# Edge indices loaded first, constants and the first normalization moved into the third counting pass

## The chip, the core and the metric

The kernel runs on one core of a Trainium2 chip, as one launch. The metric is the device time of that core in microseconds, the median of three runs.

The engines are named as in the profile: PE is TensorE (matmuls), PEld its weight loads, DVE is VectorE, ACT is ScalarE, POOL is GpSimd, SP is SyncE, which here only issues transfers. Each engine works through its own queue of instructions in order; an instruction whose inputs are not there holds everything behind it on that engine.

## What is computed

The reference is a network of four layers over a graph of 512 nodes with 768 features and 8704 edges. Each layer normalizes the nodes, adds a graph part and an attention-like part, and then a feed-forward part with experts:

```python
edge_index = jnp.stack([src, dst])
xn = _layernorm(x, axis=-1)
x = x + _L0_gnn_ref(xn, edge_index, edge_attr_256, ...) + _L0_mix_ref(xn[None], ...)[0]
x = x + _L0_ffn_ref(_layernorm(x, axis=-1)[None], ...)[0]
...
x = x + _L3_gnn_ref(xn, ..., src, dst) + _L3_mix_ref(xn[None], ...)[0]
x = x + _L3_ffn_ref(_layernorm(x, axis=-1)[None], ...)[0]
return x
```

The edges are drawn with replacement, so two nodes can be joined by several edges, of several types. What the graph parts need of the edges is therefore a table of counts: how many edges of each type go from node s to node d. The first stage of the kernel makes these tables, and sums the 256 features of the edges that arrive at each node.

## The kernel before

`Net.__init__` (L166 to L219) issues the load of the nodes x (L179, 1.5 MB) and of a table of small columns (L181) from GpSimd, and makes constants: an identity matrix, three stacked 32 x 32 identities `sel` (L188), the identity in bf16 `identb` (L205), a comparison mask `lower` (L214), node numbers `number` (L217, L219), matrices of ones, small columns. GpSimd fills some of them, VectorE casts or compares the others. The stages that read `sel`, `identb`, `lower` and `number` come after the counting.

`counts` (L363) makes the tables. Four loads bring the edges' sources, destinations and two types to the tile `raw` (named `so` in the profile, since it shares that buffer; L383). L384 casts all four to f32 as `ind`; L391 to L393 make from the types three weights per edge, `worth`, in which two counts share one f32 number (one of them times 4608). Edges lie 128 to a step, 68 steps in all. For each step j, VectorE compares a row of numbers 0 to 511 with the destination, which gives a one-hot tile `ohd` (L457, made once, kept for all passes), and with the source, times each of the three weights, which gives `so` (L460, three instructions, three buffers). TensorE multiplies the two and sums over the steps.

There are four counting passes: for each half of the sources (h = 0, 1), for each half of the steps (g = 0, 1). A pass has 34 steps with six matmuls each (L463, 204 matmuls) into six PSUM banks, which are first preset by a small matmul (L454). After each pass the six sums are copied out (L234 on VectorE, L236 on ScalarE, in turn), split into high and low parts (L470, L476, L477), and `features` (L402) follows for eight or nine groups: SP loads edge features (L406), ScalarE and VectorE split them into three bf16 parts (L408 to L411, two buffers each for `ea` and `part`), and TensorE multiplies them with `ohd` (L416). After the second and the fourth pass `finish` (L421) adds the halves and sends the tables to memory.

After `counts`, `tile_net` calls `net.norm(net.x, xn)` (L1817), the first normalization: for each quarter of the nodes two statistics instructions (L351), an aggregation (L352), a square root on ScalarE (L353), a reciprocal (L354), and the scaled copy (L355). L355 writes a tile that lies where the counting's tiles lie, so it can run only after them; the other instructions have no such bound. A scheduler orders each engine's queue by what is ready and by priority; so before, the statistics and the constants stood at the front of VectorE's queue, ahead of L384.

In the last stage, `ffn3` (L1570), scores go through a sigmoid on ScalarE (L1605) and are then ranked on VectorE (L1617 to L1622). A dummy sigmoid on one column (L1585) is there to have the sigmoid's table loaded ahead; as it depends only on a small constant, the scheduler had put it at the start of the program.

ScalarE also issues transfers there: the normalized rows of x go to memory as `f_there` (L1461), and three of the six transposed tiles `xnT` are copied out by it (L236).

Of the kernel before, what the change touches and what calls it, by code (L numbers as in the profile page):

```python
# [10 lines left out]
F32 = mybir.dt.float32  # L11
BF16 = mybir.dt.bfloat16
I16 = mybir.dt.int16
# [7 lines left out]
P = 128  # L21
N = 512
# [142 lines left out]
class Net:  # L165
    def __init__(self, ctx, tc, dram, at, out):  # L166
        self.tc, self.nc, self.d, self.at, self.out = tc, tc.nc, dram, at, out
        nc = self.nc
        self.cw = ExitStack()
        self.wp = self.cw.enter_context(tc.tile_pool(name="wp", bufs=6, side="right"))  # L170
        self.keep = ctx.enter_context(tc.tile_pool(name="keep", bufs=1))
        self.small = ctx.enter_context(tc.tile_pool(name="small", bufs=4))
        self.rowp = self.cw.enter_context(tc.tile_pool(name="rowp", bufs=2, side="right"))
        self.pp = ctx.enter_context(tc.tile_pool(name="pp", bufs=8, space=PSUM))
        self.dp = ctx.enter_context(tc.tile_pool(name="dp", bufs=1, space=DRAM))
        self.turn = 0
        keep = self.keep
        self.x = keep.tile([P, NT, D], F32, name="x")
        nc.gpsimd.dma_start(self.x, dram["x"].rearrange("(t p) d -> p t d", p=P))  # L179
        self.cols = keep.tile([P, dram["cols"].shape[1]], F32, name="cols")  # L180
        nc.gpsimd.dma_start(self.cols, dram["cols"])  # L181
        self.ident = keep.tile([P, P], F32, name="ident")
        make_identity(nc, self.ident)


        self.sel = keep.tile([96, 32], BF16, name="sel")
        for i in range(3):
            nc.vector.tensor_copy(self.sel[32 * i : 32 * i + 32, :], self.ident[:32, :32])  # L188
# [16 lines left out]
        nc.vector.tensor_copy(self.identb, self.ident)  # L205
        self.big0 = keep.tile([P, 1], F32, name="big0")
        nc.gpsimd.memset(self.big0, -BIG)
        self.onesb = keep.tile([P, P], BF16, name="onesb")
        nc.gpsimd.memset(self.onesb, 1.0)
        self.lower = keep.tile([P, P], BF16, name="lower")  # L210
        with tc.tile_pool(name="init", bufs=1) as ip:
            io = ip.tile([P, P], F32, name="io")
            nc.gpsimd.iota(io, pattern=[[1, P]], base=0, channel_multiplier=0, allow_small_or_imprecise_dtypes=True)
            nc.vector.tensor_scalar(self.lower, io, self.me, None, OP.is_gt)  # L214

        self.number = keep.tile([P, NT, 2], BF16, name="number")
        nc.vector.tensor_copy(self.number[:, :, 0], self.me.to_broadcast([P, NT]))  # L217
        for t in range(NT):
            nc.gpsimd.memset(self.number[:, t, 1:2], float(t * P))  # L219


    def ps(self):
# [121 lines left out]
    def norm1(self, x, out, t):  # L344

        nc = self.nc
        st = self.small.tile([P, 2, 6], F32, name="st")
        mv = self.small.tile([P, 2], F32, name="mv")
        r = self.small.tile([P, 1], F32, name="rs")
        for h in range(2):  # L350
            nc.vector.bn_stats(st[:, h, :], x[:, t, h * HW : (h + 1) * HW])  # L351
        nc.vector.bn_aggr(mv, st)  # L352
        nc.scalar.activation(r, mv[:, 1:2], AF.Sqrt, bias=self.eps)  # L353
        nc.vector.reciprocal(r, r)  # L354
        nc.vector.tensor_scalar(out[:, t, :], x[:, t, :], mv[:, 0:1], r, OP.subtract, OP.mult)  # L355

# [6 lines left out]
    def counts(self, c0, g0):  # L363
# [10 lines left out]
        with ExitStack() as c:  # L374
# [5 lines left out]
            ind = one.tile([P, 4, EJ], F32, name="ind")  # L380
            raw = sp.tile([P, 4, EJ], I32, name="so")
            for n, a in enumerate(("src", "dst", "edge_type_3", "edge_type_4")):
                nc.gpsimd.dma_start(raw[:, n, :], d[a].rearrange("(p j) -> p j", p=P))  # L383
            nc.vector.tensor_copy(ind, raw)  # L384


# [3 lines left out]
            for n, ((e, u), (f, v)) in enumerate((((3, 0), (3, 1)), ((3, 2), (3, 3)), ((2, 0), (2, 1)))):  # L390
                nc.vector.tensor_scalar(worth[:, n, :], ind[:, f, :], float(v), BASE, OP.is_equal, OP.mult)  # L391
                nc.vector.tensor_scalar(add, ind[:, e, :], float(u), None, OP.is_equal)
                nc.vector.tensor_add(worth[:, n, :], worth[:, n, :], add)  # L393
            io = one.tile([P, N], I16, name="io")
            nc.gpsimd.iota(io, pattern=[[1, N]], base=0, channel_multiplier=0)
            below = self.rowp.tile([1, D], BF16, name="mid", bufs=1)[:, :N]
            nc.vector.memset(below, -START)
            ohd = one.tile([P, EJ, N], BF16, name="ohd")
# [3 lines left out]
            def features(q):  # L402


                ea = ep.tile([P, 2, 256], F32, name="ea")
                nc.sync.dma_start(ea, attr[:, 2 * q : 2 * q + 2, :])  # L406
                part = ep.tile([P, 3, 2, 256], BF16, name="part")
                nc.scalar.copy(part[:, 0], ea)  # L408
                nc.vector.tensor_sub(ea, ea, part[:, 0])
                nc.scalar.copy(part[:, 1], ea)  # L410
                nc.vector.tensor_sub(part[:, 2], ea, part[:, 1])  # L411
                for i in range(2):
                    j = 2 * q + i
                    for n in range(3):
                        for f in range(2):
                            nc.tensor.matmul(eft[f], part[:, n, i, f * P : (f + 1) * P], ohd[:, j, :],  # L416
                                             start=j == 0 and n == 0, stop=j == EJ - 1 and n == 2)
# [31 lines left out]
            for h in range(2):  # L449
                digit = {}  # L450
                for g in range(2):
# [3 lines left out]
                    for j in range(g * HJ, (g + 1) * HJ):  # L455
                        if h == 0:
                            nc.vector.tensor_scalar(ohd[:, j, :], io, ind[:, 1, j : j + 1], None, OP.is_equal)  # L457
                        so = sp.tile([P, 3, 256], BF16, name="so")
                        for n in range(3):
                            nc.vector.tensor_scalar(so[:, n, :], io[:, h * 256 : (h + 1) * 256], ind[:, 0, j : j + 1],  # L460
                                                    worth[:, n, j : j + 1], OP.is_equal, OP.mult)
                        for (t, n), p in acc.items():
                            nc.tensor.matmul(p, so[:, n, t * P : (t + 1) * P], ohd[:, j, :], start=False,  # L463
                                             stop=j == (g + 1) * HJ - 1)
                    for (t, n), p in acc.items():
                        s = dg.tile([P, N], F32, name="s")
                        self.copy(s, p)
                        part = dg.tile([P, N], F32, name="part")

                        nc.scalar.activation(part, s, AF.Identity, scale=1.0 / BASE, bias=self.shift)  # L470
                        lo, hi = s, part
                        if g == 0:
                            hi = dg.tile([P, N], I16, name=f"hi{t}{n}", bufs=1)
                            lo = dg.tile([P, N], I16, name=f"lo{t}{n}", bufs=1)
                            digit[t, n] = lo, hi
                        nc.vector.tensor_scalar(hi, part, MAGIC, -MAGIC, OP.add, OP.add)  # L476
                        nc.vector.scalar_tensor_tensor(lo, hi, -BASE, s, OP.mult, OP.add)  # L477
                        if g == 1:
                            finish(h, t, n, lo, hi, *digit[t, n])

                    for q in range((2 * h + g) * EJ // 8, (2 * h + g + 1) * EJ // 8):
                        features(q)
# [1087 lines left out]
    def ffn3(self, xn, xnT, there):  # L1570
# [5 lines left out]
        with ExitStack() as c:  # L1576
# [5 lines left out]
            self.wp = c.enter_context(tc.tile_pool(name="f3_w", bufs=10, side="right"))  # L1582

            first = self.small.tile([P, 1], F32, name="r3")
            nc.scalar.activation(first, self.eps, AF.Sigmoid)  # L1585
            io = one.tile([P, P], F32, name="io")
            nc.gpsimd.iota(io, pattern=[[1, P]], base=0, channel_multiplier=0, allow_small_or_imprecise_dtypes=True)
            number = one.tile([P, NT, 2], F32, name="number")
# [208 lines left out]
def tile_net(ctx, tc, dram, at, out, only=ALL):  # L1797
# [10 lines left out]
    with ExitStack() as ck, ExitStack() as c0:  # L1808
# [4 lines left out]
        with tc.tile_pool(name="L0", bufs=1) as pool:  # L1813
            xnT = pool.tile([P, KC, N], F32, name="xnT")
            with tc.tile_pool(name="L0n", bufs=1) as p2:
                xn = p2.tile([P, NT, D], F32, name="xn")
                net.norm(net.x, xn)  # L1817
                net.to_fm(xn, xnT)
            if "mix0" in only:
                net.mix0(xnT)  # L1820
# [61 lines left out]
```

## Time and profile before

| what | value |
|---|---|
| median of 3 runs | 4313.59 us (4308.73 to 4316.22) |
| profiled execution, its own time | 4315.56 us |
| its span, first to last instruction | 4313.8 us |
| granted TensorE clock, mean | 0.986 |
| first counting matmul (L463) | 26.3 us |
| first pass ends, last pass ends | 72.6 us, 287.8 us |
| first normalized transposes (L317) | 338.9 us |
| loads of weights of the last stage (Wg, Wu, Wd) | 128 each, 1152 KB each |

In the timeline a line has its start, its busy time, the engine, the program line, the operation, output and input with sizes, and a count; in brackets stands how long the engine had been idle before it and what ended that. A busy TensorE is not one at its peak rate, since matmuls are pipelined.

### The profile page before, as it was taken

How to read it: one execution, taken by the hardware profiler on the slowest of the kernel's cores; microseconds unless marked ns; L12 is line 12 of the kernel's file. 1: busy time of each engine (PE TensorE's matmuls, PEld its weight loads, DVE VectorE, ACT ScalarE, POOL GpSimd, SP SyncE). 2: the span in 40 equal slices, each digit the busy share in tenths (PEclk: the TensorE clock that was granted, in tenths of full speed). 3: DMA queues.
4: the chain of work that ended last, by engine and by line, in shares of the span. 5: the costliest groups of instructions: out<-in, count | busy, mean ns of one | idle time of the engine just before them, and what ended most of it. 6: DMA issues, size and time to landing. Idle time of an engine off the chain costs nothing. (4 is left out here: it accounts for less than half of the span.)

```text
span 4313.8 us, 40131 instructions
## 1 busy us (share of the span) xinstructions
PE 4125.5 (96%) x16376; PEld 2099.9 (49%) x16376; DVE 1305.0 (30%) x3120; ACT 650.1 (15%) x1233; POOL 270.3 (6%) x316
## 2 busy tenths in 40 slices
PE   7989999999988999999999999978989999999998
PEld 3434555554444666755644444444554444444443
DVE  7772111112332125623220101035752122122211
ACT  2121200001211223421200000012610000000000
POOL 1120000001022010000000000021100000000000
PEclk9999999999989999999999999989999999999999
DMA  3111011111047112211211111063069999999998
GB/s 110 52 62 56 22 44 66 66 55 53 20 178 269 44 63 71 99 52 46 105 43 66 44 56 55 0 255 129 12 257 419 419 420 420 420 417 420 419 421 362
DMA packets 98956, 710.30 MB, mean 165 GB/s; under 512 B 12032, under 2 KB 12097, under 8 KB 29393
## 3 DMA queue, kind: packets, MB, share of 16 engines
q1 hardware_dynamic: 77776, 601.13, 35.1%
q0 software_dynamic: 16512, 93.97, 5.8%
q10 hardware_dynamic: 4480, 12.58, 0.8%
q8 instruction: 132, 2.16, 0.2%
q14 instruction: 56, 0.45, 0.0%
HBM read 685.09 MB, written 22.54 MB: 164 GB/s over the span
## 5 line engine op out<-in xcount | busy, mean ns | idle before, releaser
L1724 PE MATMUL ps<-w,xg 128*64 128x384 f32 x3072 | 566.0, 489 | 4.2 <-DMA w<-in_f_Wg_dram 2.1
L1724 PEld LDWEIGHTS ps<-w,xg 128*64 128x64 f32 x3072 | 234.1, 137 | 296.2 <-issue 271.1
L1356 PE MATMUL ps<-aT,w 128*128 128x512 f32 x864 | 372.3, 592 | 0.0
L1740 PE MATMUL ps<-w,hT 128*64 128x384 f32 x1536 | 320.7, 490 | 7.4 <-DMA w<-in_f_Wd_dram 3.1
L312 PE MATMUL ps<-xnT,w 128*128 128x512 f32 (+1 forms) x732 | 322.6, 598 | 0.2 <-ACT xnT L236 0.2
L1356 PEld LDWEIGHTS ps<-aT,w 128*128 128x128 f32 x864 | 164.2, 190 | 203.6 <-issue 202.3
L360 DVE TENSOR_TENSOR x<-x,ps 128x384 f32<-128x384 f32 x240 | 131.6, 552 | 329.6 <-PE ps L312 259.6
L312 PE MATMUL ps<-w,xnT 128*128 128x384 f32 x672 | 221.7, 486 | 0.2 <-DVE xnT L234 0.2
L312 PEld LDWEIGHTS ps<-xnT,w 128*128 128x128 f32 (+1 forms) x732 | 134.5, 185 | 175.9 <-issue 172.4
L1740 PEld LDWEIGHTS ps<-w,hT 128*64 128x64 f32 x1536 | 131.9, 136 | 170.8 <-issue 145.0
L312 PE MATMUL ps<-w,hT 128*128 128x384 f32 x552 | 189.4, 499 | 8.8 <-ACT hT L850 8.8
L312 PE MATMUL ps<-C,parts 128*128 128x512 bf16 x864 | 188.8, 380 | 2.5 <-DVE inv L1378 2.5
L463 PE MATMUL ps<-ohd,so 128*128 128x512 bf16 x816 | 182.1, 383 | 2.8 <-DVE so L460 2.8
L312 PEld LDWEIGHTS ps<-w,xnT 128*128 128x128 f32 x672 | 127.0, 190 | 88.6 <-issue 4.8
L1366 DVE TENSOR_TENSOR aT<-inv,ps 128x512 f32<-128x512 f32 x72 | 49.4, 686 | 365.7 <-PE ps L312 365.7
L1727 ACT ACTIVATE h<-ps 128x384 f32<-128x384 f32 x64 | 31.4, 490 | 794.0 <-PE ps L1724 794.0
L1728 DVE TENSOR_TENSOR h<-h,ps 128x384 f32<-128x384 f32 x64 | 35.4, 553 | 376.5 <-PE ps L1724 369.3
L312 PEld LDWEIGHTS ps<-w,hT 128*128 128x128 f32 x552 | 105.4, 194 | 83.9 <-ACT hT L850 13.7
L312 PE MATMUL ps<-w,aT 128*128 128x384 f32 (+1 forms) x416 | 139.6, 486 | 0.5 <-DVE aT L234 0.4
L312 PEld LDWEIGHTS <-parts 128*128 128x128 bf16 x864 | 84.8, 98 | 108.1 <-issue 8.8
L312 PE MATMUL ps<-xnT,sw 128*128 128x512 f32 x288 | 136.7, 605 | 0.0
L460 DVE TENSOR_SCALAR so<-io,ind,worth 128x256 bf16<-128x256 int16 x408 | 121.7, 356 | 35.6 <-PE ps L463 35.5
(487 smaller groups left out, 4787.7 us busy)
## 6 DMA issues: line engine op xcount, KB each, us to landing
w<-in_f_Wg_dram SPq DMA_DIRECT2D x128, 1152.0 KB, 14.5
w<-in_f_Wu_dram SPq DMA_DIRECT2D x128, 1152.0 KB, 14.4
w<-in_f_Wd_dram SPq DMA_DIRECT2D x128, 1152.0 KB, 15.2
w<-in_g_w_dram SPq DMA_DIRECT2D x54, 1152.0 KB, 5.1
w<-in_m_wqkv_dram SPq DMA_DIRECT2D x24, 1152.0 KB, 6.7
w<-in_g_t_dram SPq DMA_DIRECT2D x12, 1152.0 KB, 5.6
w<-in_m_wp_dram SPq DMA_DIRECT2D x8, 1152.0 KB, 5.3
ea<-in_edge_attr_dram SPq DMA_DIRECT2D x34, 256.0 KB, 2.7
```

What stands on the lines that cost most here:

```text
L312: self.nc.tensor.matmul(out, a, b, start=n == 0, stop=n == len(pairs) - 1)
L360: self.nc.vector.tensor_add(xs, xs, p)
L460: nc.vector.tensor_scalar(so[:, n, :], io[:, h * 256 : (h + 1) * 256], ind[:, 0, j : j + 1], worth[:, n, j : j + 1], OP.is_equal, OP.mult)
L463: nc.tensor.matmul(p, so[:, n, t * P : (t + 1) * P], ohd[:, j, :], start=False, stop=j == (g + 1) * HJ - 1)
L1356: nc.tensor.matmul(outs[nb * 3 + f], w[:, k, f * P : (f + 1) * P], xT[:, k, :], start=first and k == 0, stop=last and k == KC - 1)
L1366: nc.vector.tensor_mul(aT[:, f, :], inv[:, r, :], p)
L1724: nc.tensor.matmul(p[a * 64 : a * 64 + 64, :HW], xg[:, k, a * CAP : (a + 1) * CAP], ws[b][a][:, k, :], start=k == 0, stop=k == KC - 1)
L1727: nc.scalar.activation(h, pg[:, :HW], AF.Silu)
L1728: nc.vector.tensor_mul(h, h, pu[:, :HW])
L1740: nc.tensor.matmul(po[nb][a * 64 : a * 64 + 64, :HW], hT[:, f * P + a * 64 : f * P + a * 64 + 64], wd[a][:, f, nb * HW : (nb + 1) * HW], s ...
```

## The change

Four things are changed.

- The four index loads are issued by SP (src and edge_type_3) and ScalarE (dst and edge_type_4) in place of GpSimd. In both queues they stand first.
- GpSimd makes the matrix of ones `onesb` and the row of numbers `io` before it issues the loads of x and of the columns. `io` is one tile of 512 int16 for all uses; the separate f32 row of 128 for `lower` and the row in `counts` are gone.
- The VectorE instructions that make `sel`, `identb`, `lower` and `number` are in a new function `constants`. It and the first normalization are put behind the last `so` instruction of the third pass (h = 1, g = 0) and the last second-part copy issued until then (`issue_after`). In the queue of VectorE the constants then stand directly behind that `so`, the statistics between the evacuation of the third pass and the features that follow; of ScalarE's four roots and the load of their table likewise. The scaled copies L355 stay where they were.
- The dummy sigmoid is put behind the last root of the last normalization.

On TensorE the order of matmuls changes in two places: two of the first features' matmuls come after the first pass in place of inside it, and after the third pass some presets and the first four matmuls of the fourth pass stand among the features. On the other engines nothing behind the first normalization changes but the place of the dummy sigmoid, with its table load, which replaces the one at L1605.

```diff
         self.x = keep.tile([P, NT, D], F32, name="x")
+        self.cols = keep.tile([P, dram["cols"].shape[1]], F32, name="cols")
+
+        self.onesb = keep.tile([P, P], BF16, name="onesb")
+        nc.gpsimd.memset(self.onesb, 1.0)
+        self.io = keep.tile([P, N], I16, name="io")
+        nc.gpsimd.iota(self.io, pattern=[[1, N]], base=0, channel_multiplier=0)
         nc.gpsimd.dma_start(self.x, dram["x"].rearrange("(t p) d -> p t d", p=P))
-        self.cols = keep.tile([P, dram["cols"].shape[1]], F32, name="cols")
         nc.gpsimd.dma_start(self.cols, dram["cols"])
...
-        for i in range(3):
-            nc.vector.tensor_copy(self.sel[32 * i : 32 * i + 32, :], self.ident[:32, :32])
...
-        nc.vector.tensor_copy(self.identb, self.ident)
...
-        self.onesb = keep.tile([P, P], BF16, name="onesb")
-        nc.gpsimd.memset(self.onesb, 1.0)
...
-            io = ip.tile([P, P], F32, name="io")
-            nc.gpsimd.iota(io, pattern=[[1, P]], base=0, channel_multiplier=0, allow_small_or_imprecise_dtypes=True)
-            nc.vector.tensor_scalar(self.lower, io, self.me, None, OP.is_gt)
...
-        nc.vector.tensor_copy(self.number[:, :, 0], self.me.to_broadcast([P, NT]))
...
+    def constants(self):
+
+        nc = self.nc
+        for i in range(3):
+            nc.vector.tensor_copy(self.sel[32 * i : 32 * i + 32, :], self.ident[:32, :32])
+        nc.vector.tensor_copy(self.identb, self.ident)
+        nc.vector.tensor_scalar(self.lower, self.io[:, :P], self.me, None, OP.is_gt)
+        nc.vector.tensor_copy(self.number[:, :, 0], self.me.to_broadcast([P, NT]))
...
-        nc.scalar.activation(r, mv[:, 1:2], AF.Sqrt, bias=self.eps)
+        self.root = nc.scalar.activation(r, mv[:, 1:2], AF.Sqrt, bias=self.eps).ins
...
-                nc.gpsimd.dma_start(raw[:, n, :], d[a].rearrange("(p j) -> p j", p=P))
+                (nc.sync, nc.scalar)[n % 2].dma_start(raw[:, n, :], d[a].rearrange("(p j) -> p j", p=P))
...
-            io = one.tile([P, N], I16, name="io")
-            nc.gpsimd.iota(io, pattern=[[1, N]], base=0, channel_multiplier=0)
+            io = self.io
...
-                nc.scalar.copy(part[:, 1], ea)
+                made["part"] = nc.scalar.copy(part[:, 1], ea)
...
-                            nc.vector.tensor_scalar(so[:, n, :], io[:, h * 256 : (h + 1) * 256], ind[:, 0, j : j + 1],
+                            made["so"] = nc.vector.tensor_scalar(so[:, n, :], io[:, h * 256 : (h + 1) * 256], ind[:, 0, j : j + 1],
...
+                    if h == 1 and g == 0:
+
+                        self.begun = made["so"].ins, made["part"].ins
...
-            nc.scalar.activation(first, self.eps, AF.Sigmoid)
+            with self.tc.issue_after(self.root):
+                nc.scalar.activation(first, self.eps, AF.Sigmoid)
...
-                net.norm(net.x, xn)
+                with tc.issue_after(net.begun[0]), tc.issue_after(net.begun[1]):
+                    net.constants()
+                    net.norm(net.x, xn)
```

More of the change, by code (lines that the diff above doesn't have):

```diff
@@ L204, in __init__ @@
         self.identb = keep.tile([P, P], BF16, name="identb")
-        nc.vector.tensor_copy(self.identb, self.ident)
         self.big0 = keep.tile([P, 1], F32, name="big0")
         nc.gpsimd.memset(self.big0, -BIG)
-        self.onesb = keep.tile([P, P], BF16, name="onesb")
-        nc.gpsimd.memset(self.onesb, 1.0)
         self.lower = keep.tile([P, P], BF16, name="lower")
-        with tc.tile_pool(name="init", bufs=1) as ip:
-            io = ip.tile([P, P], F32, name="io")
-            nc.gpsimd.iota(io, pattern=[[1, P]], base=0, channel_multiplier=0, allow_small_or_imprecise_dtypes=True)
-            nc.vector.tensor_scalar(self.lower, io, self.me, None, OP.is_gt)
         self.number = keep.tile([P, NT, 2], BF16, name="number")
-        nc.vector.tensor_copy(self.number[:, :, 0], self.me.to_broadcast([P, NT]))
         for t in range(NT):
             nc.gpsimd.memset(self.number[:, t, 1:2], float(t * P))
+    def constants(self):
[5 more added lines that the diff above has]
+        nc.vector.tensor_copy(self.number[:, :, 0], self.me.to_broadcast([P, NT]))
     def ps(self):
```

## The prediction

> **What bounds the kernel now.** I read the table of engines first, then the chain of waits, then a table of stretches over the first 342 us, then the timeline of those stretches.
>
> ```profile
> PE 4125.5 (96%) x16376; PEld 2099.9 (49%) x16376; DVE 1305.0 (30%) x3120; ACT 650.1 (15%) x1233; POOL 270.3 (6%) x316
> ```
>
> TensorE is busy for 96% of the span, so a change pays where TensorE has nothing to do. The stretches show where that is in the part that the change touches (columns: stretch, length, busy time of PE, PEld, DVE, ACT and POOL, granted clock, DMA share, GB/s):
>
> ```profile
> 0.00:25.50 25.50, 2.73 (x6) 0.80 (x7) 12.48 (x36) 7.59 (x12) 13.27 (x32) 1.00 0.93 352
> 25.50:72.60 47.10, 47.09 (x208) 20.09 (x208) 46.11 (x179) 0.59 (x1) 0.00 (x0) 1.00 0.04 16
> 179.00:217.60 38.60, 38.60 (x181) 17.47 (x180) 26.27 (x90) 1.90 (x4) 0.00 (x0) 1.00 0.06 16
> 217.60:249.30 31.70, 29.23 (x129) 11.64 (x127) 24.16 (x42) 14.32 (x24) 7.75 (x8) 1.00 0.23 67
> ```
>
> The first 25.5 us hold six preset matmuls, 2.73 us. From there the counting passes keep TensorE full: the first to 72.6, the third to 217.6. Between the third and the fourth (217.6 to 249.3) it loses 31.70 - 29.23 = 2.5 us, and VectorE is busy for 24.16 of 31.70. The timeline of the start says what TensorE waits for:
>
> ```profile
> 16.09 1.48 DVE L351 BATCH_NORM_STATS2 st<-x 128x6 f32<-128x384 f32 x3 [9.15 <-DMA x<-in_x_dram]
> ...
> 20.24 1.97 DVE L188 CAST sel<-ident 32x32 bf16<-32x32 f32 x3
> ...
> 22.23 1.56 DVE L205 CAST identb<-ident 128x128 bf16<-128x128 f32 x1
> ...
> 24.23 0.28 DVE L384 CAST ind<-so 128x272 f32<-128x272 int32 x1
> ...
> 25.51 1.01 PE L416 MATMUL ps<-ohd,part 128*128 128x512 bf16 x2 [17.17 <-DVE ohd L457]
> ```
>
> VectorE stands 9.15 us on the 1.5 MB of x, then does the nodes' statistics and the constants, and only then the indices (24.23), their one-hot rows (L457, 25.11), and the first counting matmul. Nothing before L384 is needed by the counting. One other place is touched, at the start of the last stage:
>
> ```profile
> 3179.18 1.28 ACT L1605 ACT_TABLE_LOAD   x1 [5.72 <-issue]
> 3180.47 0.22 ACT L1605 ACTIVATE sc<-ps 128x64 f32<-128x64 f32 x1
> ...
> 3180.75 1.09 PE L317 MATMUL ps<-ident,sc 128*128 128x128 f32 x8 [1.64 <-ACT sc L1605]
> ```
>
> ScalarE loads the sigmoid's table when the scores are already there, and the ranking waits for it. The dummy sigmoid of L1585, meant for this, ran at 20.67 us.
>
> **The Trainium skill.** "ScalarE: Activation LUTs", What ACT_TABLE_LOAD costs, gives about 1283 ns for a load of any set; the trace has 1283 ns, ten times for L353 alone. "DMA: Bandwidth & Descriptors", Issuing engine by pattern, calls the sync and scalar queues generally faster than GpSimd's; here a 256 KB load from SP took 2.7 us in the median, the four 34 KB index loads from GpSimd 10.9 to 11.6 us, but these stood behind x. Its Specifications ask for 512 B per descriptor for full rate; an index row has 68 x 4 = 272 B, and no row of this trace shows such rows alone on a hardware queue. "GPSIMD Engine Reference", 1. Specifications, says that GpSimd's memory interfaces are shared with VectorE; the trace agrees: 18 instructions of L460 beside GpSimd's bias work took 8.02 us at 244.56, 0.446 each, and 0.86 for three, 0.287, elsewhere.
>
> **Part 1, the indices first.** SP and ScalarE each issue two of the four index loads before everything else. An SP issue takes 0.42 (0.85 for two), so src and edge_type_3 leave at 0.73 and 1.15, dst and edge_type_4 at about 0.72 and 1.1. At the 2.7 us of the first edge features they land by 3.8; this is an estimate from that row, with 1.7 (the 3 KB rows' median) and 12.0 us (the slowest features load, behind weights) as its ends. Behind them on SP the features move by 2 x 0.42 and land at 3.46 + 0.84 = 4.3; g_we and the weights move likewise, needed first at 328. ScalarE's table load moves by about 0.8, to end near 2.9, before 4.3. On GpSimd the ones and the 512-wide iota (0.20 and 0.59) go ahead of x and cols, needed first at 215 and 331 now.
>
> The order of VectorE's queue is: L384, nine instructions of worth (24.54 to 26.63 less the L457 and L460 between them, 1.05 us), L409 twice, L411 twice, then the first L457. L384 has a new wait on two queues, and everything named stands behind it. So 3.8 + 0.3 + 1.05 = 5.1; the features' pair, there at 4.3 plus 0.65 for L408, ends 2.82 us after it begins (4.11 to 6.93 before): 7.9. First one-hot at 7.9 where it was 25.1: 17.2 us earlier. TensorE's half-speed start costs the same as before (matmuls 0.43 apart from 25.5 to 29.2, 0.217 after). The loop orders two matmuls of L416 after the pass which stood in it. I take -17.0, with -18.5 (indices and features sooner) and -13.0 (indices at 8).
>
> GpSimd's bias work (L269, L270, 18.69 to 23.7) stays, but now falls into the first pass: 5 us at 0.287/0.446 costs VectorE 1.8 us. Three tiles of so, 3 x 1.30 us of matmuls, cover it: nothing, 1.8 if VectorE has no lead.
>
> **Part 2, constants and normalization after the last so of the third pass.** That so is done at 214.77 of the old clock. Behind it now: sel, identb, lower, number, which took 3.74 us (20.24 to 23.98), with GpSimd working beside them to 23.7. In the third pass GpSimd does nothing (its L271 waits until 241), so I price them at the 0.20 between L214 and L217: six, 1.2 us. The statistics run from 16.09 to 20.24, 4.15, plus 0.25 for reciprocals: 4.4. Together 5.6 us, at most 8.1. ScalarE gets one table load and four roots: 1.28 + 4 x 0.29 = 2.4; a root waits for its statistics, and behind it stand L470 and L408.
>
> VectorE's idle time from 214.77 to 249.30 is 2 x 0.44 + 31.70 - 24.16 = 8.4 us, enough in sum but mostly after 229. Before that, constants and first statistics (1.2 + 1.0) less 0.88 idle push the evacuation of the six sums by 1.3; the further statistics among L409 and L411 add 0.7, 0.6 and 1.2: the third later features group is some 3.8 us late. Features go through two buffers (L408 at 230.17, 235.73, 241.17: 5.5 us for two groups, where TensorE needs 24 x 0.217 = 5.2), so a delay is handed on; one later idle of 0.68 between L409 and L411 takes part of it. The 2.05 us that TensorE lost after 245.4 come back only in part, since GpSimd's L271 to L273 now run beside the features. I take +3.0; the ends are 0 (all in idle time) and +8.0 (all on the path). The statistics leave no gap where they were: nothing else stood before L384.
>
> **Part 3, the sigmoid's table.** The dummy now follows the last root (3170.45). 1.28 go from the path at 3179. The dummy's 1.28 + 0.20 stand ahead of the last f_there issue (3171.39) and three copies of xnT (3171.89): those move by about 0.5, and the gate's six-step sums by up to 0.4. SP's next loads wait 6.3 us for f_there, but are covered by queued weights (DMA share 1.01 from 3175 to 3200). The next weights wait for TensorE's first experts (DMA 0.11 in 3200 to 3205), so time gained here reaches the end: -0.9, ends -1.3 and 0.
>
> **Sum.** -17.0 + 3.0 - 0.9 = -14.9. The profiled execution took 4315.56, its span 4313.8 (1.8 around it): 4300.7 for it. It is 2.0 above the median 4313.59, so the median goes to 4298.7; I say 4299. Beyond 342 us only the sigmoid's place differs in the five engines' orders, so an earlier start carries through.
>
> **Rivals.** *The features ring takes it all*: VectorE has no useful idle time before 229; against it, most of the added work falls later. -17.0 + 8.0 - 0.9 = -9.9: 4303.7.
>
> *Late indices*: the short rows land after 12 us. Then L384 at 13.1, worth to 14.4, the features' pair 2.8: 17.2, a gain of 7.9, net -5.8: 4307.8. For it: 272 B rows, four queues' worth of traffic at 352 GB/s. Against: they are first on idle engines.
>
> *Slower, the ring at half speed*: if each L409 and L411 had to wait for a root or a statistic, and each statistic for ScalarE, the two-group period would go from 5.5 to 11 us; four periods cost 22: -17.0 + 22.0 - 0.9 = +4.1, 4317.7. It decides from a period of 10.0, where 4 x 4.5 eats the 17.9 gained. Against it: only a few of the later features instructions have one in front.
>
> *The move doesn't happen*: a scheduler could have placed the constants early again; the queue's order shows them after the so's, so I give that nothing.
>
> **Numbers.** Forecast 0.75, ring takes all 0.13, late indices 0.08, ring at half speed 0.04. About 0.2%, 8.6 us, can be told from no change: faster below 4305. Faster: 0.75 + two thirds of 0.13 = 0.84; same 0.12; slower 0.04. The range takes the bounds together: -18.5 + 0 - 1.3 = -19.8 and -13.0 + 7.0 - 0 = -6.0: 4293 to 4308, which holds the first two cases and half of the third.
>
> **What would show it.** First L457 at 7 to 9 us and counting matmuls from 8.2 to 55 without a gap; L384 waiting on an index DMA that lands before 5. Casts of sel near 0.2 each, not 0.66, after 195. From the end of the third pass to the fourth pass's steady run, 34 to 36 us where it was 31.7. No table load at L1605. It is wrong if L384 starts after 8, if TensorE's loss in that stretch is above 8 us, or if the shift measured at 342 us is not there at 3160.

## The result, and the profile after

The median is 4300.56 us (4295.38 to 4303.31, 11 runs) where the kernel before took 4312.43 beside it on the same chip (4307.29 to 4316.22, 11 runs): ratio 0.9974, 95% interval 0.9965 to 0.9982. That is 11.9 us less, with 8 to 15 from the interval. A second measurement of the same kernel gave 4301.86 against 4309.53, ratio 0.998 (0.9971 to 0.9988): 7.7 us less, with 5 to 12.5 from its interval. The forecast was 14.9 us less.

The profiled execution of the changed kernel took 4295.38 us, its span is 4293.4, so its profile lies 20.4 us below that of before: 9.7 at the first transposes, 7.3 between these and the last stage, 1.4 from there to the experts, 2.0 after. Only the first and the third are used below; experiment 8 says why the second is not, and the last stays open.

The first line of the page answers to the one shown of before:

```profile
PE 4115.2 (96%) x16376; PEld 2091.7 (49%) x16376; DVE 1304.4 (30%) x3120; ACT 648.2 (15%) x1232; POOL 269.9 (6%) x311
```

Work and shares are as they were. Stretches of the changed kernel that answer to those of before (stretch, length, busy time of PE, PEld, DVE, ACT and POOL, clock, DMA share, GB/s):

```profile
0.00:11.40 11.40, 2.71 (x6) 0.89 (x7) 4.89 (x15) 3.65 (x5) 5.82 (x23) 1.00 0.82 293
11.40:62.90 51.50, 50.18 (x206) 18.43 (x206) 50.24 (x178) 0.79 (x2) 4.96 (x4) 1.00 0.30 124
...
208.10:239.80 31.70, 29.80 (x130) 11.77 (x129) 27.82 (x62) 16.73 (x29) 9.61 (x8) 1.00 0.23 60
```

The empty start is 11.4 us long instead of 25.1. But the first pass, which took 47.5 us from the first one-hot row before, takes 51.5, and has 4.96 us of GpSimd work in it where it had none. The stretch after the third pass, with the constants and statistics now in it, is no worse: TensorE is busy for 29.80 of 31.70 us, before for 29.23, although VectorE's busy time there rose from 24.16 to 27.82.

The timeline of the start (the lines of the changed kernel stand 3 to 7 further down: L388 is L384 of before, L411 to L414 are L408 to L411, L460 is L457, L463 is L460, L466 is L463):

```profile
0.73 0.41 ACTq L387 DMA_DIRECT2D so<-in_dst_dram  x1
0.73 0.38 SPq L387 DMA_DIRECT2D so<-in_src_dram  x1
...
1.49 0.93 POOL L185 DMA_DIRECT2D x<-in_x_dram  x1
1.64 0.90 SPq L409 DMA_DIRECT2D ea<-in_edge_attr_dram  x2
...
4.23 0.43 DVE L388 CAST ind<-so 128x272 f32<-128x272 int32 x1 [2.85 <-DMA so<-in_edge_type_dram]
...
6.25 0.68 DVE L412 TENSOR_TENSOR ea<-ea,part 128x512 f32<-128x512 f32 x1
8.79 0.62 ACT L411 CAST part<-ea 128x512 bf16<-128x512 f32 x1 [3.24 <-DMA ea<-in_edge_attr_dram]
...
9.44 0.69 DVE L412 TENSOR_TENSOR ea<-ea,part 128x512 f32<-128x512 f32 x1 [2.51 <-ACT part L411]
10.05 1.46 DVE L414 TENSOR_TENSOR part<-ea,part 128x512 bf16<-128x512 f32 x2
...
11.43 0.35 DVE L460 TENSOR_SCALAR ohd<-io,ind 128x512 bf16<-128x512 int16 x1
```

The indices are there at 4.2 and the weights `worth` at 6.25, so a one-hot row could begin then. The time of `worth` does not hang on the landing of the indices. In a second profile of the same kernel (experiment 8) they are there 0.7 us earlier:

```profile
3.49 1.16 DVE L388 CAST ind<-so 128x272 f32<-128x272 int32 x1 [2.12 <-DMA so<-in_edge_type_dram]
```

The cast takes 1.16 us in place of 0.43, and ends at 4.66 in both profiles, 0.16 after GpSimd's fill of `bias`, which runs from 3.09 to 4.50 in both; VectorE's next work after `worth` begins at 6.25 and 6.24.

In VectorE's queue the first two features groups stand ahead of it. The second group's load, which landed in time before, can be used only from 8.79; ScalarE splits it, VectorE subtracts, and the first one-hot row comes at 11.43.

Milestones in us (a pass ends with the last matmul of its long row):

| kernel | first one-hot row | first pass ends | third ends | first transposes |
|---|---|---|---|---|
| before | 25.11 | 72.62 | 217.76 | 338.87 |
| changed | 11.43 | 62.91 | 208.29 | 329.19 |

13.7 us are gained at the first one-hot row, 9.7 at the end of the first pass, and 9.7 at the first transposes.

### The profile page after: what moved, and what is told of

Same layout as the page of the kernel before. It is cut to its first block, busy times and chain, and to the rows that moved or that the text cites. A ratio compares the mean times of both kernels' runs of the same rounds, so it can differ in the third digit from the quotient of the medians.

```text
span 4293.4 us, 40119 instructions
## 1 busy us (share of the span) xinstructions
PE 4115.2 (96%) x16376; PEld 2091.7 (49%) x16376; DVE 1304.4 (30%) x3120; ACT 648.2 (15%) x1232; POOL 269.9 (6%) x311
## 5 line engine op out<-in xcount | busy, mean ns | idle before, releaser
L466 PE MATMUL ps<-ohd,so 128*128 128x512 bf16 x816 | 184.3, 383 | 2.6 <-DVE so L463 2.5
L1734 ACT ACTIVATE h<-ps 128x384 f32<-128x384 f32 x64 | 31.4, 491 | 793.7 <-PE ps L1731 793.7
L466 PEld LDWEIGHTS <-so 128*128 128x128 bf16 x816 | 77.8, 98 | 115.0 <-DVE so L463 28.7
```

The lines of the kernel that those rows point to most:

```text
L1734: nc.scalar.activation(h, pg[:, :HW], AF.Silu)
```

## Experiments

Each kernel is the changed one with an edit. Each was timed beside the kernel before on the same chip (4310.65 us for experiments 1 to 4, 4309.94 for 5 to 8, 4309.53 for the last two runs), and is compared through it. Lines of an edited kernel may be shifted by one to eight.

| experiment | first one-hot row | first pass ends | third ends | first transposes | median | ratio to before |
|---|---|---|---|---|---|---|
| 1 bias work later | 12.00 | 59.53 | 205.80 | 326.43 | 4297.69 | 0.997 (0.9959 to 0.9981) |
| 2 one-hot rows spread | 11.46 | 59.52 | 204.90 | 325.72 | 4296.21 | 0.9967 (0.9955 to 0.998) |
| 3 features later | 6.25 | 57.96 | 203.98 | 324.75 | 4293.36 | 0.9961 (0.9947 to 0.9974) |
| 4 all three | 6.25 | 53.41 | 200.69 | 321.51 | 4292.41 | 0.9959 (0.9946 to 0.9973) |
| 5 x issued later | 8.33 | 60.40 | 205.71 | 326.30 | 4298.77 | 0.9974 (0.9964 to 0.9984) |
| 6 indices as before | 19.19 | 70.51 | 215.96 | 336.57 | 4308.14 | 0.9999 (0.999 to 1.0008) |
| 7 constants not held | 11.38 | 64.50 | 211.41 | 332.39 | 4304.44 | 0.9984 (0.9977 to 0.9991) |
| 8 sigmoid as before | 11.34 | 62.90 | 208.25 | 329.96 | 4302.27 | 0.9983 (0.9976 to 0.9989) |

### 1. GpSimd's bias work out of the first pass

Why does the first pass take 4 us longer? The timeline of the changed kernel, VectorE's and GpSimd's lines:

```profile
11.69 0.85 DVE L463 TENSOR_SCALAR so<-io,ind,worth 128x256 bf16<-128x256 int16 x3
...
12.72 1.49 DVE L463 TENSOR_SCALAR so<-io,ind,worth 128x256 bf16<-128x256 int16 x3
13.31 0.81 POOL L273 CAST bias<-row 1x768 bf16<-1x768 f32 x1 [6.92 <-DMA row<-in_m_bv_dram]
14.21 1.75 POOL L274 TENSOR_TENSOR row<-row,bias 1x768 f32<-1x768 f32 x1
...
14.39 4.13 DVE L463 TENSOR_SCALAR so<-io,ind,worth 128x256 bf16<-128x256 int16 x3
15.92 0.81 POOL L273 CAST bias<-row 1x768 bf16<-1x768 f32 x1
16.81 1.63 POOL L274 TENSOR_TENSOR row<-row,bias 1x768 f32<-1x768 f32 x1
```

Three `so` instructions take 0.85 us alone; beside GpSimd's subtractions they take 4.13, and the triple before 1.49. The excess is 3.28 + 0.64 = 3.9 us. The experiment lets GpSimd's arithmetic on the bias rows begin only after a tile of the second pass:

```diff
-        self.parts(out, t[:1, :n], t[:1, :n], mid[:, :n], [self.nc.gpsimd.tensor_copy] * 3, self.nc.gpsimd.tensor_sub)
+        with self.tc.issue_after(self.gate):
+            self.parts(out, t[:1, :n], t[:1, :n], mid[:, :n], [self.nc.gpsimd.tensor_copy] * 3, self.nc.gpsimd.tensor_sub)
...
+                        if h == 0 and j == HJ + 5:
+                            gate = self.small.tile([1, 1], BF16, name="gate")
+                            self.gate = nc.gpsimd.tensor_copy(gate, so[:1, 0, :1]).ins
```

> GpSimd's arithmetic on the two bias rows is held until the second counting pass; all else is as in the changed kernel. GpSimd theory (its bias work at 13.3 to 18.5 us keeps VectorE from the so tiles, and VectorE has no slack in the first pass): the first pass ends near 58.9 us instead of 62.75, the median falls by 3 to 4 us to about 4297. Pace theory (VectorE's own queue, with the one-hot rows of all 68 steps in the first pass, sets the pace, and GpSimd beside it adds little): the pass still ends at 62 or later, median 4300. Traffic theory (the 400 GB/s of x and weights until 25 us slow the engines): no change either, since the transfers stay.

In its timeline the third triple, and with it all others of the pass, is back at 0.85:

```profile
14.32 0.85 DVE L464 TENSOR_SCALAR so<-io,ind,worth 128x256 bf16<-128x256 int16 x3
```

The pass takes 59.53 - 12.00 = 47.5 us, as in the kernel before. So the 4.0 us go with GpSimd's work: the loads beside the pass and the earlier start are still there without it. One more thing differs between the profiles. TensorE's matmuls stand 0.43 us apart at first and 0.22 later, and this slow start lasts 3.7 us before, 5.7 in the changed kernel and 3.9 here. It is not what made the pass longer: in the second profile of the changed kernel it lasts 4.2, and the pass takes 51.4 all the same. Of the 4.0 us, 2.8 are left at the first transposes; 0.6 went into a later first row, and the stretch from the first to the third pass's end is 0.9 longer, where the bias work now lies.

### 2. The same bias work, with room beside it

The program makes the one-hot rows of the second pass ahead, in the first: two or three `ohd` rows between the triples. Here each row waits for the `so` of the step before it, so that a pass makes only its own:

```diff
-                            nc.vector.tensor_scalar(ohd[:, j, :], io, ind[:, 1, j : j + 1], None, OP.is_equal)
+                            with tc.issue_after(made["so"].ins) if j else ExitStack():
+                                nc.vector.tensor_scalar(ohd[:, j, :], io, ind[:, 1, j : j + 1], None, OP.is_equal)
```

> Each one-hot row is queued behind the so of the step before, so that only 34 of 68 are made in the first pass. GpSimd's bias work stays where it is. GpSimd theory and pace theory both: VectorE gets 6 to 9 us of slack in the first pass and makes up for the loss; the pass ends near 58.5 us instead of 62.75, the second pass stays at about 44 us, median near 4297. Traffic theory: the pass still ends at 62.5.

The collision is all there, in the timeline of this kernel:

```profile
15.26 1.75 POOL L274 TENSOR_TENSOR row<-row,bias 1x768 f32<-1x768 f32 x1
...
15.44 4.14 DVE L464 TENSOR_SCALAR so<-io,ind,worth 128x256 bf16<-128x256 int16 x3
```

Yet the pass takes 48.1 us. VectorE's busy time in it is 43.8 us of 48.1, against 50.2 of 51.5 in the changed kernel. So nearly all that the collision costs the pass, it costs because rows that nobody needs yet have taken VectorE's spare time. Here TensorE idles 0.21 us once, at 19.63, and then runs 116 matmuls in 25.64 us, 0.221 each; in the changed kernel it idles 0.57 and 0.27 and then runs 108 in 25.40, 0.235 each, at VectorE's pace.

### 3. The first features behind step 20

```diff
-                nc.vector.tensor_sub(ea, ea, part[:, 0])
-                made["part"] = nc.scalar.copy(part[:, 1], ea)
-                nc.vector.tensor_sub(part[:, 2], ea, part[:, 1])
+                with tc.issue_after(made["early"]) if q < 2 else ExitStack():
+                    nc.vector.tensor_sub(ea, ea, part[:, 0])
+                    made["part"] = nc.scalar.copy(part[:, 1], ea)
+                    nc.vector.tensor_sub(part[:, 2], ea, part[:, 1])
...
+                        if h == 0 and j == 20:
+                            made["early"] = made["so"].ins
```

> VectorE's and ScalarE's splits of the first two features groups are queued behind step 20 of the first pass. Theory that the first one-hot row waits in VectorE's queue behind these four instructions, and they wait for the second features load, landing at 8.8 us: first one-hot row at 6.3 us in place of 11.4. As the pass is bound by VectorE, only the wait of 2.5 us is saved, not the 2.9 us of work: the pass ends near 60.3 us, median about 4298. Rival, that TensorE alone bounds the pass: it ends 5 us sooner, at 57.7, median 4295.5. If the index loads themselves were late, the first one-hot row stays at 11.

The first row comes at 6.25, straight after `worth`, 5.2 us earlier; so those 5.2 us were the features' pair: 2.5 of waiting for the second load, the rest its work. The pass ends at 57.96, near the rival's 57.7, not at my 60.3: I had expected the pair's 2.8 us of VectorE to be paid later in the same pass. VectorE is busy for all 51.7 us from the first row to the pass's end, where in the changed kernel 1.3 of 51.5 are idle. What took up the rest of the 2.8 was not tried.

### 4. All three edits

> The three together. If the three causes are right and TensorE is then the bound of the first pass: first one-hot row at 6.3 us, pass ended at 53 to 54.5 us, 8 to 9.5 us sooner than in the changed kernel, median 4291 to 4293. If something else holds the pass, transfers or TensorE's half-speed start, it ends at 57 or later and the median is 4296 or more.

First row at 6.25, and the pass takes 47.2 us. The transposes come 7.7 us before those of the changed kernel, 17.4 before those of the kernel before. It consists of the three edits above and nothing else. It was run again beside the unaltered changed kernel:

> The version with all three edits (bias arithmetic in the second pass, one-hot rows one step ahead, first features' splits behind step 20), beside the changed kernel in one job. Transposes stand 7.7 us earlier than in the changed kernel (321.5), and nothing later differs in order: the median is 7 to 8 lower than the changed kernel's of this job, 17 to 19 lower than the kernel before. If the gain is lost downstream, less than 4.

Median 4290.61 (4290.23 to 4292.13), ratio to before 0.9957 (0.9943 to 0.997), where the changed kernel has 4301.86 and 0.998 (0.9971 to 0.9988). The two medians are 11.2 apart, more than the 7 to 8 expected, the two profiles' transposes 8.8 (320.34 and 329.12). I take the transposes for the edits' effect, since nothing later differs in order. They have a spread of their own: the two profiles of this version differ by 1.2 us there (321.51 and 320.34). The first row is at 6.25 in both, but TensorE's slow start lasts 4.8 us in one and 2.9 in the other, and at half the pace 1.9 us more cost about 0.95, which is the difference at the end of the first pass (53.41 and 52.47). This version beats both kernels: in this measurement its five runs all lie below every run of the two.

### 5. x issued behind GpSimd's constants

Was it x that held up the second features load? The 1.5 MB are issued at 3.79 here instead of 1.49:

```diff
-        nc.gpsimd.dma_start(self.x, dram["x"].rearrange("(t p) d -> p t d", p=P))
-        nc.gpsimd.dma_start(self.cols, dram["cols"])
...
             nc.gpsimd.memset(self.number[:, t, 1:2], float(t * P))
+        nc.gpsimd.dma_start(self.x, dram["x"].rearrange("(t p) d -> p t d", p=P))
+        nc.gpsimd.dma_start(self.cols, dram["cols"])
```

> The changed kernel, but GpSimd issues x and cols after its constants, at about 4 to 4.5 us instead of 1.49; nothing else moves. Theory (the second features load lands at 8.7 instead of 4.3 because the 1.5 MB of x, issued before it, shares the DMA engines with it): both features loads land by about 5.0, their pair is done by 8, first one-hot at 7.9 to 9.0, and the first pass ends 2.5 to 3.5 us earlier than 62.9. Rival (the weights behind it on the same queue, or the index loads ahead of it, hold it): lands at 8.0 or later, first one-hot at 10.8 to 11.5, first pass end as it was.

The timeline of its start:

```profile
3.70 0.30 DVE L388 CAST ind<-so 128x272 f32<-128x272 int32 x1 [2.32 <-DMA so<-in_edge_type_dram]
...
4.89 1.33 ACT L411 CAST part<-ea 128x512 bf16<-128x512 f32 x2 [1.96 <-DMA ea<-in_edge_attr_dram]
...
8.33 0.35 DVE L460 TENSOR_SCALAR ohd<-io,ind 128x512 bf16<-128x512 int16 x1
```

Both features tiles are split in one row, from 4.89, and the first one-hot row stands at 8.33. The weights are issued at 2.58 in both kernels, so it was x that held up the second load. Not all of the 3.1 us at the first row are x's. With x issued later, GpSimd's fill of `bias` ends at 2.99 in place of 4.50, the cast L388 takes 0.30, and the features' pair begins at 5.75 in place of 6.25. About 0.5 us are therefore GpSimd's constants and 2.6 x, an estimate from these starts. The end of the pass follows by 2.5 us; GpSimd's collision is still in it (52.1 us from row to end), and the profile has TensorE once more at a granted clock of 0.50, from 24.15 to 27.57, which the others don't have; if TensorE was the limit there, up to 1.7 us of the pass are due to it. The median doesn't show the 2.9 us at the transposes: 11.2 below before, where the changed kernel has 11.9 and 7.7 in its two measurements; 3 us are within that spread.

### 6. The index loads on GpSimd again, behind x

```diff
-                (nc.sync, nc.scalar)[n % 2].dma_start(raw[:, n, :], d[a].rearrange("(p j) -> p j", p=P))
+                nc.gpsimd.dma_start(raw[:, n, :], d[a].rearrange("(p j) -> p j", p=P))
```

> The changed kernel, but the four index loads are issued by GpSimd again, behind x, cols and its constants, as before the change; constants and statistics stay in the third pass. VectorE's queue then has the features' pair first and the indices after it. Theory (both halves of the change are needed: with 1.5 MB of x ahead the indices land 11 us after an issue at about 5.4 to 6.5, so at 17 to 18): the indices are converted at 17 to 18, first one-hot at 18 to 19, where the changed kernel has 11.43 and the kernel before 25.11; first pass ends 5 to 7 us later than the changed kernel's 62.9, at 68 to 70; median about 4306. Rival (moving VectorE's work alone brings it all, the index loads land in time anyway because the features' pair was late): first one-hot at 11.5 to 12.5, median as the changed kernel.

```profile
17.65 0.30 DVE L388 CAST ind<-so 128x272 f32<-128x272 int32 x1 [10.75 <-DMA so<-in_edge_type_dram]
```

That line of its timeline has VectorE idle for 10.75 us until the indices land at 17.65. The first row comes at 19.19 and the pass ends at 70.51, both a little later than expected; the pass has GpSimd's collision in it as well (51.3 us from row to end). The transposes come 2.3 us before those of the kernel before. So taking the constants and statistics from the front, without the early loads, is worth 2.3 us; the other 7.4 of the changed kernel's 9.7 need the early loads too. Its time can't be told from that of the kernel before.

### 7. Constants and statistics not held for the third pass

```diff
-                with tc.issue_after(net.begun[0]), tc.issue_after(net.begun[1]):
-                    net.constants()
-                    net.norm(net.x, xn)
+                net.constants()
+                net.norm(net.x, xn)
```

> The changed kernel, but constants and statistics are not held for the third pass; they then stand among the last one-hot rows of the first pass (constants and eight statistics before its last evacuation) and two statistics among the features of the second pass. Theory (hidden work: the third/fourth boundary cost nothing because VectorE had lead and idle time there; in the last rows of the first pass no new ohd rows are made, so it idles 0.44 of every 1.3 us): 6.4 us of work against about 2.2 us of idle time plus the lead of the buffers of so, so that TensorE waits 1 to 4 us near 60 us; first pass ends at 64 to 67 instead of 62.9 or the same amount goes into the next boundary, and the stretch from third-pass end to fourth-pass end stays at 69.9. Rival (place doesn't matter at all, only that the work is not before the first pass): first pass ends at 62.9 and the first transposes of the nodes stand at 329.2. Second rival (the move into the third pass is what makes the time; work at a pass without idle VectorE is paid in full): 6.4 us, transposes at 335.

The scheduler then puts them among the last rows of the first pass and the features behind it. TensorE's timeline there:

```profile
58.06 4.14 PE L466 MATMUL ps<-ohd,so 128*128 128x512 bf16 x18 [0.36 <-DVE so L463]
62.95 1.55 PE L466 MATMUL ps<-ohd,so 128*128 128x512 bf16 x6 [0.75 <-DVE so L463]
```

The pass ends 1.6 us later, the third pass 3.1, the transposes 3.2. So the third pass is the better place by 3.2 us, about half of the work, as the first of the expected theories had it. This kernel also has the stretch behind the third pass without the added work: it takes 70.00 us from the third pass's end to the fourth's (211.41 to 281.41), with it 69.89, before 70.18. Why the added 3.7 us of VectorE show no cost can be read, though no experiment isolates it, when TensorE's losses there are set side by side. Without the added work, from this kernel's timeline:

```profile
235.59 1.96 POOL L276 TENSOR_TENSOR bias<-row,mid 1x768 bf16<-1x768 f32 x1
...
238.92 1.76 PE L466 MATMUL ps<-ohd,so 128*128 128x512 bf16 x7 [0.31 <-DVE so L463]
241.95 0.39 PE L466 MATMUL ps<-ohd,so 128*128 128x512 bf16 x1 [1.26 <-DVE so L463]
242.82 19.38 PE L466 MATMUL ps<-ohd,so 128*128 128x512 bf16 x89 [0.48 <-DVE so L463]
```

And with it, in the changed kernel:

```profile
222.89 1.36 POOL L275 CAST mid<-row 1x768 bf16<-1x768 f32 x1 [61.80 <-PE ps L457]
...
226.57 5.45 PE L419 MATMUL ps<-ohd,part 128*128 128x512 bf16 x22 [0.84 <-DVE part L414]
232.38 2.62 PE L419 MATMUL ps<-ohd,part 128*128 128x512 bf16 x10 [0.36 <-ACT part L413]
234.85 15.49 PE L466 MATMUL ps<-ohd,so 128*128 128x512 bf16 x71
```

In the first, GpSimd's second bias job starts with the last presets (234.69) and collides with the fourth pass's `so`: 0.31 + 1.26 + 0.48 = 2.05 us of TensorE. In the second, the presets stand earlier, the last of them among the features at 222.43; GpSimd starts with it at 222.89, collides with the features, and is done before the `so` begin; TensorE loses 0.84 + 0.36 and, earlier, 0.28. One loss takes the place of the other. That holds for this order and does not make the work free: in experiment 8, whose features stand in another order with the same work, the stretch takes 70.8 us.

### 8. The sigmoid's table as before, and the same kernel again

```diff
-            with self.tc.issue_after(self.root):
-                nc.scalar.activation(first, self.eps, AF.Sigmoid)
+            nc.scalar.activation(first, self.eps, AF.Sigmoid)
```

> The changed kernel with one part undone: the dummy sigmoid stands at its old place, at the start, not behind the last square root. Theory (the 1.38 us gained in the last stage are the table load that left the path): a table load of 1.28 us stands again at the sigmoid of the scores, and from the first transpose of the last stage to the first matmul of the experts it takes 32.0 us, as before the change, where the changed kernel takes 30.64; the median is about 1.4 above the changed kernel's 4300.6 if runs could tell that. Rival (the gain in that stage is a difference between two profiles, like the 7 us between 342 and 3160): 30.6 with the load on the path or without it.

The timeline of the changed kernel:

```profile
3153.47 1.28 ACT L1592 ACT_TABLE_LOAD   x1
...
3162.19 0.22 ACT L1612 ACTIVATE sc<-ps 128x64 f32<-128x64 f32 x1 [5.74 <-issue]
...
3175.18 7.06 PE L316 MATMUL ps<-oh,xn 128*128 128x128 f32 x48 [6.47 <-DVE oh L1638]
```

With the dummy back in its old place:

```profile
3165.62 1.28 ACT L1611 ACT_TABLE_LOAD   x1 [5.72 <-issue]
...
3179.90 7.17 PE L316 MATMUL ps<-oh,xn 128*128 128x128 f32 x48 [6.47 <-DVE oh L1637]
```

From the first transposes of the stage (3151.53 and 3154.98) to the gathering matmuls of `oh` it is 23.65 us with the change, 24.92 without it, 24.91 in the kernel before (3168.53 to 3193.44). The difference, 1.27, is the load of 1.28. Up to the experts the two differ by 1.37, but no more than the 1.27 is shown to be an effect: experiments 1, 5 and 6, with the changed kernel's order there, have 31.3 to 31.4 to the experts instead of 30.64. In experiment 1 the difference lies in the 48 gathering matmuls, which took 7.76 us at a granted clock of 0.71, where the changed kernel's took 7.06 at 0.78. This kernel's transposes are 0.8 us later than the changed kernel's, because the scheduler set the features after the third pass in another order (TensorE waits 0.30, 0.36, 0.62 and 1.25 there).

> The changed kernel itself, once more, unaltered. If the changed kernel's profile gained 7 us between 342 and 3160 us by chance of its execution, this profile's first transposes stand at 329.2 within 0.3, as in the changed kernel's first profile, and the time from them to the last stage may differ by up to 8 us from its 2822.3; if that stretch is a property of the kernel, it repeats at 2822 within 1. Median 4300 within 3.

The unaltered kernel's second profile has the transposes at 329.12 again, but 2827.1 us from there to the last stage's, where the first had 2822.3 and the profile of before 2829.7. The 7.3 us of the two profiles are therefore not evidence for the change: the same program differs by 4.8 from itself.

## Why the prediction was right in its sum and wrong in its terms

The total, -14.9, and the measured -11.9 agree within the interval, if barely, and the forecast of 4299 lies 1.6 below the median. The second measurement, 7.7 less with 5 to 12.5, leaves -14.9 out, and the terms as measured below make -11.3. So the sum was forecast some 3 to 7 us too large. The terms:

- **Start, -17.0 taken (-18.5 to -13.0): it is -9.7, outside its range.** Three steps failed, and a fourth was wrong without a cost.
  - *Indices.* "They land by 3.8", worth at 5.1; it was 6.25, 1.15 late. The landing is not what failed: L388 began at 4.23 in one profile of the changed kernel and at 3.49 in the other, and ended at 4.66 in both. The failed step is the price "0.3 + 1.05", taken from a time when GpSimd did nothing. Now the cast and `worth` run beside GpSimd's constants, and the cast ends just after GpSimd's fill of `bias` in all nine profiles in which x is issued ahead of that fill and the indices come early; where the fill is earlier (experiment 5), the cast takes 0.30.
  - *Features.* "Behind them on SP the features move by 2 x 0.42 and land at 3.46 + 0.84 = 4.3": I moved a landing time by the later issue and forgot what the same change puts between them. Before, both loads were issued at 0.73, x at 1.29. Now x, at 1.49, is ahead of the features at 1.64, and the second of them lands 6.7 us after its issue. Experiment 5 takes x away and gets 8.33 for the first row, 0.4 from the 7.9 forecast. Of 3.5 us of error 3.1 go with that edit, about 2.6 with x itself.
  - *GpSimd's bias work.* "Three tiles of so ... cover it: nothing, 1.8 if VectorE has no lead." It cost 4.0. The price was from a mean: 18 instructions in 8.02 us, 0.446 each, as if they were all slowed. GpSimd's work beside that row ended at 249.2 and the row began at 244.56, so its excess of 8.02 - 18 x 0.287 = 2.9 us fell in 4.6 us. And the cover was not there: VectorE's 46.11 busy of 47.10, which the prediction itself showed for this pass, says that little more than 1 us hides in it (experiments 1 and 2).
  - *TensorE's slow start.* It "costs the same as before": it lasted 3.7 us before, and 5.7 and 4.2 in the two profiles of the changed kernel, so it can't be counted on to be the same. In the changed kernel VectorE was the limit, and it cost nothing that shows (51.5 and 51.4 us for the pass).
- **Boundary of third and fourth pass, +3.0 taken (0 to +8.0): it is -0.3.** The parts went as said: the constants took 0.92 us from 205.22 (1.2 priced; `sel` 0.53 for three, near 0.2 each), the root's table load is at 214.67. The step that failed is "come back only in part": the 2.05 us of the old collision came back whole, and the price of the new one with the features, 1.5 us, was smaller. Delays were not handed on as 3.8 us. That rests on reading the traces (experiment 7) and on the order that the scheduler happened to choose.
- **Sigmoid, -0.9 taken (-1.3 to 0): it is -1.27.** The 0.4 set against it, for the later copies of `xnT`, did not arise: from the transposes to the first gate matmul it is 4.00 us in the changed kernel and in experiment 8.
- Of the signs set out, L388 on an index DMA that lands before 5, the short `sel` casts, no load at the sigmoid and a shift of 342 that is still there at 3160 are seen. Three are not: the first row at 7 to 9, counting matmuls without a gap to 55 (TensorE idles at 18.0 and 19.6), and a longer stretch behind the third pass.

7.3 us of missing gain at the start, 3.3 of missing loss later and 0.4 at the end make 3.6; the sum comes out near by luck of signs. The range's upper end also has a slip: it adds +7.0 for the boundary, whose end was given as +8.0; with that it would be 4309 and not 4308. Of the rivals, "late indices" had the right shape, a load that lands late at the start, but named the wrong load. The two on the features ring didn't come: ScalarE's L411 comes back to the same buffer, two groups on, after 7.4 us once (219.55 to 226.93) and then after 5.5 (to 232.46), far from 11.

## What to carry to other kernels

When a load is moved to the front, list again what every queue now issues before each of the other early loads: one of 256 KB that was first and landed in time is not the same load once 1.5 MB stand before it. A start that is moved earlier also slides onto work that stays where it was, so look up which engines come to overlap, price the work as it runs beside the other engine, and read from the busy time of that stretch whether it has room. Room can be made by taking out what is done ahead of need, which here was worth no less than removing the collision itself.

## What the runs showed of the hardware

- A GpSimd subtraction over one partition of 768 numbers (1.63 to 1.75 us) holds up a VectorE instruction of 0.28 us for about its own length: three, beside two subtractions and a cast, take 4.13 us. The Trainium skill, "SBUF — State Buffer", Who interferes with whom, describes the port pair that the two engines share as an exclusive lock, for VectorE instructions in a two-port mode or with two inputs in SBUF: whoever issues first has it for the whole instruction and the other "fully blocks". The trace agrees with the block: the three end at 16.05, 16.82 and 18.53, each 0.09 after the GpSimd instruction beside it. The mean of 0.446 that the prediction used hid it. A fill does the same: the cast L388 took 1.16 us beside GpSimd's fill of `bias` and 0.30 without it.
- Four index loads with rows of 272 B on SP and ScalarE's queues, 34 KB each, were usable 2.3 to 3.1 us after the last issue at 1.17 (from 3.49 to 4.23 in nine profiles with 1.5 MB of x issued at 1.49, at 3.70 in the one with x later). On GpSimd's queue behind x they were usable at 17.65, some 10 to 12 us after their issues (5.53 to 7.68).
- A features load of 256 KB lands in 2.7 us in the median. With x issued at 1.49, the load at 1.64 could be used at 4.93, and the next, issued at 2.10, only at 8.79, 6.7 us after its issue.
- TensorE's matmuls of 512 columns stood 0.43 us apart after the idle start and 0.22 later. How long the slow start lasts differs between profiles of one program: 4.8 and 2.9 us for the version of experiment 4, 5.7 and 4.2 for the changed kernel.
